# Storing a dense fallback's output from another DMA queue, in a kernel that takes the other branch

## The chip, the core and the metric

The kernel runs on one core of one Trainium2 chip. Its metric is the device time of one execution in microseconds (us), as the median of several runs. The core's engines, by the names that the profile uses, are PE (the matrix unit), PEld (its weight loads), DVE (the vector engine), ACT (the scalar engine), POOL (GpSimd) and SP (SyncE, which here only issues DMAs and waits). A name with a "q" behind it (POOLq, SPq) is that engine's sequencer, which runs waits, branches and the like.

## What is computed

Two graph layers on 3327 nodes with 512 features and a sparse symmetric adjacency matrix whose diagonal is one. Each layer adds its result to its input and normalises the rows. Layer 0 is graph attention with four heads; layer 1 mixes an attention sum with a plain neighbour sum through two gates:

```python
x, adj                                                # (3327, 512), (3327, 3327) of zeros and ones
# layer 0, for each head h
feats = x @ W[h]
logits = leaky_relu(e_self[:, None] + e_neigh[None, :], 0.2), adj == 0 masked
g0 = relu(softmax(logits) @ feats + b[h])
x = layernorm(x + g0)
# layer 1
h = x @ W_sa
e = where(adj != 0, exp(-leaky_relu(s_left[:, None] + s_right[None, :], 0.01)), 0)
x_a = (e / (e.sum(1) + 1e-5)) @ h
x_b = adj @ (x @ W_gcnb) + b_gcnb
g1 = sigmoid(attn_a * x_a + attn_b * x_b)             # attn_a, attn_b: sigmoids of row sums
x = layernorm(x + g1)
```

## The kernel before

The function `gat_then_gated_gnn` (L1445) has two ways to compute this. `sparse_pass` (L80) always runs. It turns each node's row of the adjacency matrix into a list of at most a few dozen neighbours, gathers those neighbours' rows and sums them with weights. While it does so it also tests whether the lists hold every neighbour; `covered` (L509) writes the answer into `flag`, a single word in on-chip memory (L523). Then comes `with tc.If(... flag ... > 0)` (L1450): if some list had overflowed, `dense_pass` (L1068) would compute everything anew from the whole matrix. With the inputs at hand the lists hold all neighbours, the flag is 0, and no instruction of `dense_pass` appears in the profile. It is a fallback that is built into the program and not run.

`sparse_pass` works on 26 tiles of 128 nodes. A first stage (until about 240 us in the profile) loads the adjacency matrix and the features from SP's queue, computes layer 0's feature rows (L351) into a table in DRAM, and makes the lists on DVE. A second stage (until about 660 us) is layer 0: POOL gathers table rows with indirect DMAs (L615), DVE and ACT weigh them, and PE sums them by multiplying with the identity (L763). The third stage is layer 1, with gathers again from L615, sums on DVE (L967) and PE (L988), and a projection (L1007). Finished rows are normalised on ACT (L1052, up to four tiles at a time) and put into the output with an indirect DMA from POOL, through this helper:

```python
def scatter(group, dst, rows, src, last=None):                    # L143
    put = nc.gpsimd.indirect_dma_start(                           # L145
        out=dst, out_offset=bass.IndirectOffsetOnAxis(ap=rows, axis=0), in_=src, in_offset=None,
        bounds_check=last, oob_is_err=last is None,
    ).ins
    ...
scatter("out", out, own(order[k]), z, N - 1)                      # L1055, 26 times
```

The order of the work is written out by hand, engine by engine; a layer above adds the semaphores. It counts each engine's finished instructions on one semaphore (`Pool_49`, `DVE_49` and so on), the DMAs issued by SP and ACT on eight semaphores `DMAHW0_49` to `DMAHW7_49` in turn, and the DMAs issued by POOL on eight more, `DMASW0_49` to `DMASW7_49`. Every finished DMA adds 16 to its semaphore.

Behind the branch the two ways join, and from there each semaphore must stand at the same value whichever way was taken. So the built program holds, beside the block with `dense_pass` (the true block), a second block that has no line of its own in the source (the false block; its instructions carry L1450). In it each engine adds to its semaphores what the true block would have added. For POOL the false block of the kernel before has seven instructions:

1. a semaphore instruction that waits until `Pool_49` reaches 63 and adds 67 to it;
2. four semaphore instructions that wait until `DMASW1_49` to `DMASW7_49` have reached the counts of all POOL DMAs issued so far;
3. an instruction that waits for `DMASW0_49` in the same way and then raises all eight, by 48 (six of them) or 64 (two). The profile calls it INC_SWDGE_SEM. (48 is three DMAs, 64 is four: 26 stores of `dense_pass`, L1442, dealt over eight semaphores.)
4. a branch to the block behind the join.

SP's false block has eight semaphore instructions, one for each of `DMAHW0_49` to `DMAHW7_49`; ACT, PE and DVE have one each.

The block behind the join (its instructions carry L1514) ends the program. SP waits for all sixteen DMA semaphores and the engines' own at their final values, runs two DRAIN instructions [...] and reports to a barrier. ACT, PE and DVE run a DRAIN and report too. POOL runs a DRAIN, collects the four reports, releases the others, runs a second DRAIN, clears the semaphores (EVENT_SEMAPHORE_RANGE_CLEAR), runs a third DRAIN and holds a second barrier of the same kind. Its end is the end of the execution.

Of the kernel before, what the change touches and what calls it, by code (L numbers as in the profile page):

```python
# [14 lines left out]
P = 128  # L15
# [1052 lines left out]
def dense_pass(  # L1068
# [21 lines left out]
    nc = tc.nc  # L1090
# [6 lines left out]
    def rows(t):  # L1097
        return min(P, N - t * P)
# [39 lines left out]
    x1 = x1_pool.tile([P, NT, F], F32, name="x1")  # L1138
# [25 lines left out]
    with tc.tile_pool(name="feats", bufs=1) as feats_pool:  # L1164
# [3 lines left out]
        with tc.tile_pool(name="p0", bufs=1) as p0, tc.tile_pool(name="p0s", bufs=2) as p0s, tc.tile_pool(  # L1168
# [16 lines left out]
            for c0 in range(0, N, CH):  # L1185
# [3 lines left out]
                for t in range(c0 // P, (c0 + cw + P - 1) // P):  # L1189
                    r, o = rows(t), t * P - c0  # L1190
# [19 lines left out]
            for t in range(NT):  # L1210
                r = rows(t)
# [24 lines left out]
        with tc.tile_pool(name="m0", bufs=2) as m0p, tc.tile_pool(name="m0o", bufs=1, space=PSUM) as pso, tc.tile_pool(  # L1236
            name="m0t", bufs=2, space=PSUM
        ) as pst:
            for n0 in range(0, N, NB):
# [3 lines left out]
                for j, t in enumerate(tiles):  # L1243
                    r = rows(t)
# [7 lines left out]
                for t0, g in groups(G):  # L1252
# [4 lines left out]
                    for t in range(t0, t0 + g):  # L1257
                        r = rows(t)
# [30 lines left out]
                for j, t in enumerate(tiles):  # L1289
                    r = rows(t)  # L1290
# [31 lines left out]
    with tc.tile_pool(name="p1", bufs=1) as p1, tc.tile_pool(name="p1s", bufs=2) as p1s, tc.tile_pool(  # L1322
# [19 lines left out]
        for t in range(NT):  # L1342
            r = rows(t)
# [24 lines left out]
    with tc.tile_pool(name="m1", bufs=2) as m1p, tc.tile_pool(name="m1o", bufs=1, space=PSUM) as pso, tc.tile_pool(  # L1368
        name="m1t", bufs=2, space=PSUM
    ) as pst:  # L1370
        for n0 in range(0, N, NB):
# [3 lines left out]
            for j, t in enumerate(tiles):  # L1375
                r = rows(t)
# [9 lines left out]
            for t0, g in groups(G):  # L1386
                at = m1p.tile([P, G, NB], F32, tag="at", name=f"at{n0}_{t0}")
                load_adjT(at, t0, g, n0, nw)
                for t in range(t0, t0 + g):
                    r = rows(t)  # L1390
# [22 lines left out]
            for j, t in enumerate(tiles):  # L1413
                r = rows(t)
# [24 lines left out]
            normalise(m1p, f"b{n0}", tiles, stats)  # L1439
            for t in tiles:  # L1440
                r = rows(t)
                nc.gpsimd.dma_start(out[t * P : t * P + r, :], x1[:r, t, :])  # L1442


def gat_then_gated_gnn(tc, x, xT, xB, xL, adj, adjT, adjB, adjL, diag, xo, W0, W0B, b0, a_self, a_neigh, *rest):  # L1445
    N = adj.shape[0]
    with tc.tile_pool(name="flag", bufs=1) as pool:
        flag = pool.tile([1, 1], I32, name="flag")
        sparse_pass(tc, flag, x, xB, xL, adjB, adjL, diag, xo, W0B, b0, a_self, a_neigh, *rest)
        with tc.If(tc.nc.values_load(flag[0:1, 0:1]) > 0):  # L1450
            dense_pass(tc, x[:N], xT, adj, adjT, W0, b0, a_self, a_neigh, *rest)
# [65 lines left out]
```

## Time and profile before

| what | us |
|---|---|
| median of three runs | 974.06 |
| lowest and highest of them | 973.56, 977.38 |
| the profiled execution's own time | 1108.9 |
| span of the profiled execution, first to last instruction | 1107.2 |

The profiled execution is longer than that median by 1108.9 - 974.06 = 134.8 us. All durations below come from it, and times of day ("at 1094") are microseconds from its start.

By stages the engines were busy as follows (us of busy time in the stage; the clock is what was granted to PE, as a share of full speed; the last column is the mean busy share of the core's DMA engines):

| stage | length | PE | DVE | ACT | POOL | clock | DMA |
|---|---|---|---|---|---|---|---|
| 0 to 240: lists and layer 0's features | 240.0 | 135.35 | 143.90 | 31.56 | 97.36 | 0.78 | 0.83 |
| 240 to 660: layer 0 | 420.0 | 326.46 | 233.34 | 135.87 | 252.84 | 0.85 | 0.62 |
| 660 to 720: layer 1 begins | 60.0 | 36.09 | 26.34 | 8.99 | 43.48 | 0.68 | 0.70 |
| 720 to 1094.9: layer 1 | 374.9 | 332.20 | 313.34 | 102.48 | 229.62 | 0.95 | 0.53 |

What is left, from 1094.9 to 1107.2, is the end of the program.

Three views of the profile are used below. The view by source line lists every kind of instruction that a line gave, on engines and sequencers, with its shortest, median and longest duration in ns and the start of the first and last of them in us. The view by windows gives the busy time and number of instructions of each engine in a stretch of time. The view of waits adds up who waited for whom; its releasers are inferred from semaphores.

### The profile page before, as it was taken

Reading aid. Unit: us, or ns where it says so; the run is one execution under the profiler, and the core shown is the slowest. Engines: PE = TensorE matmul, PEld = TensorE weight load, DVE = VectorE, ACT = ScalarE, POOL = GpSimd, SP = SyncE. Lnnn points to the kernel's source line nnn. Section 1 sums busy time; section 2 is a strip of 40 time slices with the busy share of each in tenths; the row PEclk is TensorE's granted clock in tenths of the full one; section 3 lists DMA queues with packets and bytes.
Section 4 is the critical chain, followed back from the end, with each engine's and each line's share of the span. In section 5 each row is a group of like instructions: output and inputs, shape, how many; then the busy total and the mean of one; then the engine's idle time right before and its main releaser. Section 6 shows DMA issues by size and latency. Waiting matters only on the chain.

```text
span 1107.2 us, 10091 instructions
## 1 busy us (share of the span) xinstructions
PE 830.1 (75%) x2534; PEld 435.9 (39%) x2534; DVE 716.9 (65%) x2118; ACT 278.9 (25%) x820; POOL 623.3 (56%) x664
## 2 busy tenths in 40 slices
PE   4499973028768697868848976689898989697992
PEld 3377751014334343434424432244344434343441
DVE  4286786187333673855536655398797989968872
ACT  1022120004221442433313421122222222131331
POOL 7410247607675466466766437737777777776311
PEclk9698995557778898989979985889898999898997
DMA  9899899603976567486766417726676576766200
GB/s 324 316 359 399 346 321 381 198 0 105 394 232 173 149 204 206 147 307 197 213 187 202 145 62 200 204 77 190 178 191 185 173 193 174 189 177 180 76 29 31
DMA packets 74243, 221.88 MB, mean 200 GB/s; under 512 B 14944, under 2 KB 19216, under 8 KB 73280
## 3 DMA queue, kind: packets, MB, share of 16 engines
q0 software_dynamic: 47008, 153.87, 47.1%
q1 hardware_dynamic: 24512, 65.17, 15.6%
q10 hardware_dynamic: 2656, 2.10, 0.6%
q8 instruction: 23, 0.38, 0.1%
q14 instruction: 44, 0.36, 0.1%
HBM read 200.01 MB, written 28.55 MB: 206 GB/s over the span
## 4 chain that ended last, share of the span: by engine, by line
PE 40%; issue 16%; POOL 12%; DVE 12%; another core or an unknown queue 9%; DMA 5%; ACT 5%; ACTq 0%; DVEq 0%; POOLq 0%; SPq 0%
PE acc L763 12%; PE pf L351 7%; POOL g L615 7%; PE po L1007 6%; PE acc L988 6%; PE pcol L787 2%; DMA g<-table,srt 2%; DMA at<-in_adjB 2%; PE acc L752 2%; DVE sw L967 2%; POOL out L145 1%; ACT g L758 1%; POOL lists L145 1%; PE pt L998 1%
## 5 line engine op out<-in xcount | busy, mean ns | idle before, releaser
L615 POOL DMA_INDIRECT g<-table,srt x464 | 476.1, 1026 | 217.9 <-issue 145.8
L763 PE MATMUL acc<-g,ident 128*128 128x512 f32 x504 | 238.3, 629 | 2.4 <-issue 2.4
L967 DVE SCALAR_TENSOR_TENSOR sw<-g,e,sw 128x512 f32<-128x512 f32 x226 | 169.4, 750 | 13.5 <-ACT sw L951 6.2
L763 PEld LDWEIGHTS acc<-g,ident 128*128 128x128 f32 x504 | 103.5, 206 | 139.8 <-issue 126.8
L988 PE MATMUL acc<-g,ident 128*128 128x512 f32 x262 | 126.4, 617 | 13.5 <-DMA g<-table,srt 9.5
L1007 PE MATMUL po<-wsa,sT 128*128 128x512 f32 x208 | 101.4, 633 | 18.3 <-issue 13.3
L351 PE MATMUL pf<-w,xc 128*128 128x260 f32 x416 | 103.4, 411 | 13.4 <-DVE w L291 13.4
L760 DVE TENSOR_TENSOR g<-g,w 128x512 f32<-128x512 f32 x176 | 109.7, 692 | 0.6
L351 PEld LDWEIGHTS pf<-w,xc 128*128 128x128 f32 x416 | 84.7, 206 | 29.4 <-DVE w L291 13.9
L1007 PE MATMUL po<-wg,sT 128*128 128x512 f32 x208 | 93.7, 593 | 0.0
L758 ACT ACTIVATE g<-g,w 128x128 f32<-128x128 f32 x304 | 91.9, 390 | 2.7 <-issue 2.2
L787 PE MATMUL pcol<-v,xt 128*128 128x8 f32 x208 | 35.7, 299 | 74.1 <-ACT xt L784 57.1
L988 PEld LDWEIGHTS acc<-g,ident 128*128 128x128 f32 x262 | 51.0, 197 | 82.6 <-issue 54.0
L1007 PEld LDWEIGHTS po<-wsa,sT 128*128 128x128 f32 x208 | 42.3, 206 | 77.3 <-issue 67.4
L969 DVE TENSOR_TENSOR g<-g 128x512 f32<-128x512 f32 x95 | 65.7, 692 | 3.3
L787 PEld LDWEIGHTS pcol<-v,xt 128*128 128x128 f32 x208 | 33.3, 244 | 80.6 <-ACT xt L784 62.0
L361 POOL DMA_DIRECT2D table<-row x26 | 14.4, 555 | 87.5 <-ACT st L360 87.5
L145 POOL DMA_INDIRECT out<-za,srt x26 | 28.8, 1108 | 57.2 <-ACT za L1052 51.1
L1007 PEld LDWEIGHTS po<-wg,sT 128*128 128x128 f32 x208 | 39.4, 190 | 48.8 <-issue 48.0
L1000 ACT COPY sT<-pt 128x512 f32<-128x512 f32 x52 | 29.1, 587 | 113.5 <-remote 56.7
L379 PE MATMUL pc<-at,pow 128*32 128x512 bf16 (+1 forms) x182 | 23.9, 434 | 36.7 <-DMA at<-in_adjB 20.2
L784 ACT COPY xt<-x1t 128x512 f32<-128x512 f32 x26 | 15.2, 584 | 141.0 <-PE x1t L780 74.9
(236 smaller groups left out, 934.3 us busy)
## 6 DMA issues: line engine op xcount, KB each, us to landing
at<-in_adjB SPq DMA_DIRECT2D x78, 512.0 KB
g<-table,srt POOLq DMA_INDIRECT x464
table<-row POOLq DMA_DIRECT2D x26, 260.0 KB
xc<-in_xB SPq DMA_DIRECT2D x6, 1024.0 KB
own<-in_xo SPq DMA_DIRECT2D x1, 3640.0 KB
own<-table SPq DMA_DIRECT2D x1, 3640.0 KB
at<-in_adjL SPq DMA_DIRECT2D x13, 256.0 KB
table<-x1a SPq DMA_DIRECT2D x12, 260.0 KB
```

The costliest lines, as they stand in the source:

```text
L145: put = nc.gpsimd.indirect_dma_start(out=dst, out_offset=bass.IndirectOffsetOnAxis(ap=rows, axis=0), in_=src, in_offset=None, bounds_check ...
L351: nc.tensor.matmul(pf[:, hh, :HC], xc[:, k, o : o + P], w0[:, k, hh, :], start=(k == 0), stop=(k == KT - 1))
L615: nc.gpsimd.indirect_dma_start(out=buf[:, q - q0, :], out_offset=None, in_=table[:, :], in_offset=bass.IndirectOffsetOnAxis(ap=srt[g][:, i ...
L758: nc.scalar.activation(gv[:, h, :], gv[:, h, :], AF.Copy, scale=w[:, s, h : h + 1])
L760: nc.vector.tensor_tensor(gv, gv, w[:, s, :].rearrange("p (h o) -> p h o", o=1).to_broadcast([P, H, FO]), ALU.mult)
L763: nc.tensor.matmul(acc, ident, buf[:, o + s - s0, 0:F], start=False, stop=(s == CAPS[j] and j not in T0))
L787: nc.tensor.matmul(pcol, xt1[:, k, :], v1[:, k, :], start=(k == 0), stop=(k == KT - 1))
L967: nc.vector.scalar_tensor_tensor(sw, g[:, i, 0:F], e[:, s : s + 1], sw, ALU.mult, ALU.add)
L969: nc.vector.tensor_add(g[:, i, 0:F], g[:, i - 1, 0:F], g[:, i, 0:F])
L988: nc.tensor.matmul(plain[j], to, row, start=(not sums_of_two and i == 0), stop=(sums_of_two and i == len(rows) - 1),)
L1000: nc.scalar.copy(sT, pt)
L1007: nc.tensor.matmul(proj[j], sT[:, k, :], wt[:, k, :], start=(half + k == 0), stop=(half + k == KT))
```

## The change

One call changes its engine. The 26 stores at the end of `dense_pass`, in the block that isn't run, are issued from SP's queue and no longer from POOL's:

```diff
@@ -1439,7 +1439,7 @@
             normalise(m1p, f"b{n0}", tiles, stats)
             for t in tiles:
                 r = rows(t)
-                nc.gpsimd.dma_start(out[t * P : t * P + r, :], x1[:r, t, :])
+                nc.sync.dma_start(out[t * P : t * P + r, :], x1[:r, t, :])
```

In the built program all that runs ahead of the branch is the same, instruction by instruction, on every engine. The true block loses 44 instructions on POOL and gains 42 on SP; the stores of one block of nodes stand on SP between the second and the third load of the next block's matrix tiles. In the false block POOL keeps the first of its seven instructions (`Pool_49` by 67, as before) and the branch; the four waits and INC_SWDGE_SEM are gone. SP's false block has the same eight instructions with other amounts (608 or 624 where it had 560 or 576). The block behind the join has the same 37 instructions; SP waits there for `DMASW0_49` to `DMASW7_49` at 1184 or 1200, which are the counts of the POOL DMAs that were issued, where it waited for 1232 or 1248.

## The prediction

> **What bounds the kernel now.** The change lies behind the last tile of layer 1, so I read the end of the program first. The view by windows, for all engines, from the last scatter on (columns: window, length, busy us and number of instructions of PE, PEld, DVE, ACT and POOL, granted clock, DMA share, GB/s):
>
> ```profile
> 1094.90:1096.80 1.90, 0.00 (x0) 0.00 (x0) 0.00 (x0) 0.00 (x0) 0.00 (x0) 0.50 0.39 146
> 1096.80:1097.30 0.50, 0.00 (x0) 0.00 (x0) 0.00 (x0) 0.00 (x0) 0.00 (x0) 0.50 0.05 16
> 1097.30:1099.20 1.90, 0.00 (x0) 0.00 (x0) 0.00 (x0) 0.00 (x0) 0.00 (x0) 0.50 0.01 4
> 1099.20:1106.30 7.10, 0.00 (x0) 0.00 (x0) 0.00 (x0) 0.00 (x0) 0.00 (x0) 0.50 0.00 0
> 1106.30:1107.20 0.90, 0.00 (x0) 0.00 (x0) 0.00 (x0) 0.00 (x0) 0.00 (x0) 0.50 0.00 0
> ```
>
> No engine works after 1094.9, and from 1097.3 no data moves: the last 10 us belong to sequencers. The view of the lines of branch and join, on POOL, says what its sequencer does there:
>
> ```profile
> L1450 POOLq EVENT_SEMAPHORE  x5: 17/42/43, 1096.9 to 1097.2; - x5
> L1450 POOLq TENSOR_LOAD <-flag x1: 507/507/507, 1093.6 to 1093.6; - x1
> L1450 POOLq COMPARE_BRANCH  x1: 53/53/53, 1094.2 to 1094.2; - x1
> L1450 POOLq INC_SWDGE_SEM  x1: 1916/1916/1916, 1097.3 to 1097.3; - x1
> ...
> L1514 POOLq EVENT_SEMAPHORE  x4: 17/17/17, 1106.4 to 1107.1; - x4
> L1514 POOLq DRAIN  x3: 46/103/7093, 1099.2 to 1106.9; - x3
> L1514 POOLq EVENT_SEMAPHORE_RANGE_CLEAR  x1: 177/177/177, 1106.7 to 1106.7; - x1
> ```
>
> INC_SWDGE_SEM takes 1.92 us, and the first DRAIN behind it 7.09 us (its longest of three; the others take 0.10 and 0.05). Together 9.0 us of POOL alone. Who waits for it, in the view of waits of SP's queue over the end:
>
> ```profile
> SPq L1514 <- DMA out<-za,srt: 435.8, 1, 435.8
> SPq L1514 <- PEq L1514: 7.1, 2, 6.6
> ```
>
> SP is through its false block at 663.3 and waits 435.8 us, until 1099.1. The view names the DMA of the last output rows, yet that had landed earlier: POOL's own waits for the same semaphores were over by 1097.3. What SP waits for from then on is the raise by INC_SWDGE_SEM, for it wants 1248 where the DMAs give 1200. Then SP stands 6.6 us at the barrier. The view names PE, which had reported at 1087.4; the one still missing is POOL, in its DRAIN. Last, the scatter that ends the real work, in the view in order of time:
>
> ```profile
> 1093.87 0.99 POOL L145 DMA_INDIRECT out<-za,srt  x1 [2.07 <-ACT za L1052]
> ```
>
> [...] The last scatter's record ends at 1094.86 and its last completion came at 1096.74, 1.88 us later[...] POOL's branch ends at 1094.27 and the next instruction runs at 1096.85: 2.6 us. [...]
>
> **The change, part by part.** I lay the tail out as it stands, from the trace, and then without the removed parts.
>
> Before: scatter landed 1096.74; POOL's five semaphore instructions 1096.85 to 1097.24; INC_SWDGE_SEM 1097.28 to 1099.20; SP's twelve waits and two DRAINs 1099.14 to 1099.96 (0.82 us), beside POOL's DRAIN, 1099.23 to 1106.32; then two barriers and the clearing, to 1107.17. From the release of POOL's wait for the reports to the end it is 0.80 us.
>
> *Removed: four semaphore waits* on POOL, 0.35 us (1096.96 to 1097.28, and the gap behind). They check what SP checks again.
>
> *Removed: INC_SWDGE_SEM*, 1.92 us, on both paths, SP's and POOL's. With it SP's start goes from 1099.14 to the landing, 1096.74 plus 0.04 (the gap between the raise at 1099.10 and SP's start) = 1096.78. SP then reports at 1096.78 + 0.82 = 1097.60.
>
> *The DRAIN.* It now stands behind one semaphore instruction at 1096.85 and begins at about 1096.9. Its length is not shown without the INC in front, so I bound it. Below: 0.05 us, the shortest of the three. Above: 7.09, as before. I take the low end, at most the 0.19 us of the DRAIN at the program's start with four memsets in front of it. The reason: before it lie only DMA instructions, and those free POOL at once. Scatters at 1089.52 and 1090.81 each took 0.99 and stood 0.30 apart; a POOL that were busy 10 us with what a scatter leaves behind could not do that. What else lies between the last scatter and the DRAIN is INC_SWDGE_SEM. Against that stands one thing: the program's first lines have an instruction of that name too,
>
> ```profile
> L1504 POOLq INC_SWDGE_SEM  x1: 27/27/27, 0.2 to 0.2; - x1
> ...
> L1504 POOLq DRAIN  x1: 188/188/188, 0.4 to 0.4; - x1
> ```
>
> and neither it nor the DRAIN behind it is long. But that one only resets, carries no amounts and names no semaphore, so I don't take it for the same work. So POOL is at the barrier by 1097.1 and waits there for SP.
>
> *Next to be late* is thus SP, with its 0.82 us behind the landing. The end: 1097.60 + 0.04 + 0.80 = 1098.44. The gain is 1107.17 - 1098.44 = 8.7 us, of which the INC and POOL's waits are 2.3 (1099.10 - 1096.78) and the DRAIN the other 6.4.
>
> *Added: other amounts* in SP's eight semaphore instructions. They ran from 662.8 to 663.3, 430 us ahead of the end; that wait covers them, and without cover they would cost what they did, 0.5 us.
>
> *Moved: 26 stores*, with their DMAs, to SP, ahead of the loads of the next block's third to last matrix tiles. Each waits for DVE to finish the normalisation, and those loads queue behind it, with PE and DVE waiting for the tiles. All of it is in the block that isn't run: cost nothing, because the flag is 0. If it were run, the price would be unknown from this trace. Nothing is moved ahead of the branch, so stages up to 1094.9 keep their time.
>
> Sum: -8.7 us against the profiled execution's own 1108.9, so 1100.2. The stretch holds no matrix work and next to no DMA, so I carry it over to the median in microseconds: 974.06 - 8.7 = **965.3**. If everything in the profiled execution were stretched by 1108.9 / 974.06, the gain would be 7.7 and the time 966.4.
>
> **Rivals.** *A, forecast: the DRAIN belongs to INC_SWDGE_SEM*, 965.3. *B: the DRAIN stays.* If the 7.09 us belong to the first DRAIN behind any POOL DMAs, or to the recording, then only 2.3 us are saved: in the first case the DRAIN runs from 1096.9 to 1104.0 and the program ends at 1104.8; 974.06 - 2.3 = 971.8. For it: the only other DRAINs of POOL stand before any DMA or right behind another DRAIN. Against it: no DMA is under way in those 7 us. *C: nothing is saved.* If POOL's cores were busy until 1106.3 with something that started with the last scatter, the DRAIN would start sooner and end at the same time: 974.1. Against it speaks the 0.30 us between scatters. *D, slower: instruction fetch.* POOL's program is 49 instructions shorter between branch and end[...]. Place: POOL, between branch and DRAIN, or inside the last block. Price: 2.6 us a fetch, as behind the branch now. It decides from the first additional fetch if the DRAIN stays (974.06 - 2.3 + 2.6 = 974.4), and only from the fourth if the DRAIN goes (4 x 2.6 = 10.4 against 8.7). For it: the branch does stall today. Against it: POOL's ten last instructions are few, and three instruction fetches of 8 KB are recorded from 1096.7 to 1097.5 without a stall of that size behind them.
>
> **How the numbers follow.** A 0.70, B 0.20, C 0.07, D 0.03. A's own range is 963.5 to 967.5 (both ways of carrying over, and run to run scatter: two of the three runs shown lie within 0.5 us and the third 3.3 above). The range reaches on over B, to 972.5, and leaves out C and D, about 0.10, and the tails. A change of 0.5%, 4.9 us, is about what a measurement of this kernel can tell from none. A is faster than that (below 969.2); B, C and D lie within it: faster 0.70, same 0.28, and slower 0.02 for a D of several fetches.
>
> **What would show it.** In the profile after: no INC_SWDGE_SEM at L1450 and one semaphore instruction of POOL there; SP's wait for the output's DMA ending within 0.1 us of the landing; all three DRAINs of POOL under 0.2 us; 1.7 us from landing to end, where it was 10.4. A DRAIN of 7 us in the profile means B, whether or not the median moves as in A; a DRAIN that still ends some 9.6 us after the landing means C; a gap well over 2.6 us behind POOL's branch, or a new one further on, means D. Short DRAINs with a median near 972 would say that the 7 us were the recording's. Any difference ahead of the branch would contradict the whole reading.

## The result and the profile after

The changed kernel takes 970.57 us (median of 20 runs, 967.71 to 974.86) where the kernel before takes 974.23 (median of 20, 971.03 to 977.38). The ratio is 0.9965 with a 95% interval of 0.9953 to 0.9978: 3.4 us faster, 2.1 to 4.6. The forecast was 8.7 us.

One thing has to be known to read the traces: chips differ. On two of the chips used in the experiments the kernel before takes 975 to 978 us, on three others 1104 to 1108. Going by their lengths, the profiled execution shown before the change ran on a chip of the slower kind, the first profile after on one of the faster. So I compare tails, from the start of the last output scatter to the end of the program. The changed kernel's tail didn't depend on the chip: it was 8.93 us in a run of 969.5 us span and 8.93 us again in one of 1094.8. The scatter from which it counts, in the first of them:

```profile
960.57 0.98 POOL L145 DMA_INDIRECT out<-za,srt  x1 [2.07 <-ACT za L1052]
```

Before the change the tail was 1107.17 - 1093.87 = 13.30 us. It is thus 4.4 us shorter, within the interval of the measured gain.

The same views as before the change. The view by windows, from the start of POOL's first closing DRAIN on (busy us and number of instructions of PE, PEld, DVE, ACT, POOL, then clock, DMA share, GB/s):

```profile
961.50:963.70 2.20, 0.00 (x0) 0.00 (x0) 0.00 (x0) 0.00 (x0) 0.05 (x1) 0.50 0.35 129
963.70:964.60 0.90, 0.00 (x0) 0.00 (x0) 0.00 (x0) 0.00 (x0) 0.00 (x0) 0.50 0.00 0
964.60:968.70 4.10, 0.00 (x0) 0.00 (x0) 0.00 (x0) 0.00 (x0) 0.00 (x0) 0.50 0.00 0
968.70:969.50 0.80, 0.00 (x0) 0.00 (x0) 0.00 (x0) 0.00 (x0) 0.00 (x0) 0.50 0.00 0
```

The scatter has landed by 963.72 and SP is through with its waits by 964.6; then 4.1 us pass in which no engine works and no data move. POOL's sequencer, by the lines of the branch and of the join:

```profile
L1450 POOLq TENSOR_LOAD <-flag x1: 503/503/503, 960.3 to 960.3; - x1
L1450 POOLq COMPARE_BRANCH  x1: 50/50/50, 960.9 to 960.9; - x1
L1450 POOLq EVENT_SEMAPHORE  x1: 17/17/17, 961.4 to 961.4; - x1
...
L1514 POOLq EVENT_SEMAPHORE  x4: 17/17/17, 968.7 to 969.4; - x4
L1514 POOLq DRAIN  x3: 50/109/7158, 961.5 to 969.2; - x3
L1514 POOLq EVENT_SEMAPHORE_RANGE_CLEAR  x1: 177/177/177, 969.0 to 969.0; - x1
```

INC_SWDGE_SEM and the four waits are gone, as announced. The DRAIN is not: it takes 7.16 us with no INC_SWDGE_SEM in front of it. And the first instruction behind the branch comes 0.44 us after it (960.96 to 961.40), where it had come after 2.59. The view of waits of SP's queue over the end:

```profile
SPq L1514 <- DMA out<-za,srt: 398.3, 1, 398.3
SPq L1514 <- PEq L1514: 4.8, 2, 4.3
```

The first line now means what it says: SP waits for the landing, until 963.74. The second is again the barrier, where the one missing is POOL, still in its DRAIN: 4.3 us, where it had been 6.6.

### The profile page after: what moved, and what is told of

It reads as the page before. It is cut to its first block, busy times and chain, and to the rows that moved or that the text cites. A ratio compares the mean times of both kernels' runs of the same rounds, so it can differ in the third digit from the quotient of the medians.

```text
span 969.5 us, 10086 instructions
## 1 busy us (share of the span) xinstructions
PE 804.4 (83%) x2534; PEld 421.7 (43%) x2534; DVE 716.6 (74%) x2118; ACT 278.2 (29%) x820; POOL 626.2 (65%) x664
## 4 chain that ended last, share of the span: by engine, by line
PE 45%; DVE 19%; DMA 12%; POOL 11%; issue 7%; ACT 4%; DVEq 0%; ACTq 0%; POOLq 0%
PE acc L763 21%; PE pf L351 9%; POOL g L615 7%; DMA g<-table,srt 7%; DVE sw L967 7%; DMA at<-in_adjB 3%; PE po L1007 3%; PE pcol L787 3%; PE acc L988 3%; PE acc L752 3%; DVE g L969 2%; ACT xt L784 1%; DMA a_row<-in_a_self 1%; PE x1t L780 1%; POOL sprod L321 1%
## 5 line engine op out<-in xcount | busy, mean ns | idle before, releaser
L763 PE MATMUL acc<-g,ident 128*128 128x512 f32 x504 | 230.8, 614 | 1.4 <-DVE g L760 1.4
L763 PEld LDWEIGHTS acc<-g,ident 128*128 128x128 f32 x504 | 100.4, 199 | 132.1 <-issue 101.1
L988 PE MATMUL acc<-g,ident 128*128 128x512 f32 x262 | 128.6, 618 | 24.9 <-DVE g L969 14.7
L1007 PE MATMUL po<-wg,sT 128*128 128x512 f32 x208 | 98.0, 616 | 0.0
L1007 PE MATMUL po<-wsa,sT 128*128 128x512 f32 x208 | 95.2, 601 | 0.3 <-ACT sT L1000 0.3
L988 PEld LDWEIGHTS acc<-g,ident 128*128 128x128 f32 x262 | 49.1, 193 | 95.8 <-issue 44.7
L1037 ACT ACTIVATE za<-za 128x512 f32<-128x512 f32 x26 | 16.4, 631 | 170.8 <-DVE za L1035 170.8
L1007 PEld LDWEIGHTS po<-wsa,sT 128*128 128x128 f32 x208 | 40.2, 194 | 51.3 <-issue 48.9
L787 PE MATMUL pcol<-v,xt 128*128 128x8 f32 x208 | 32.4, 283 | 33.1 <-ACT xt L784 33.1
L787 PEld LDWEIGHTS pcol<-v,xt 128*128 128x128 f32 x208 | 30.0, 222 | 38.8 <-ACT xt L784 38.6
L717 DVE TENSOR_TENSOR w<-g,srt 128x20 f32<-128x20 f32 (+3 forms) x55 | 9.7, 184 | 48.2 <-DMA g<-table,srt 46.9
```

The lines of the kernel that those rows point to most:

```text
L763: nc.tensor.matmul(acc, ident, buf[:, o + s - s0, 0:F], start=False, stop=(s == CAPS[j] and j not in T0))
L787: nc.tensor.matmul(pcol, xt1[:, k, :], v1[:, k, :], start=(k == 0), stop=(k == KT - 1))
L988: nc.tensor.matmul(plain[j], to, row, start=(not sums_of_two and i == 0), stop=(sums_of_two and i == len(rows) - 1),)
L1007: nc.tensor.matmul(proj[j], sT[:, k, :], wt[:, k, :], start=(half + k == 0), stop=(half + k == KT))
```

## The experiments

The theory at this point: a DRAIN on POOL works off something that POOL's own DMAs leave behind. Rivals: it has a fixed price behind any POOL DMA; or the first long one in a program pays for something loaded once; or, as forecast, it belongs to INC_SWDGE_SEM.

### One DRAIN more, early (e1, g3)

```diff
                 scatter("out", out, own(order[k]), z, N - 1)
+            if k0 == 20:
+                nc.gpsimd.drain()
             ready = None
```

> The changed kernel with one DRAIN more on POOL, behind the scatters of tiles 20 to 22 of layer 1's order, where POOL then idles about 12 us; three scatters follow it. Backlog theory (a DRAIN works off something that POOL's DMAs leave behind, so its length grows with the DMAs since the last DRAIN): the early DRAIN takes about 7.1 us, hidden, the closing one under 0.5 us, the end comes about 2 us behind the last landing; 4.1 us faster than the changed kernel, near 966.5. Fixed-price theory (the first DRAIN behind any POOL DMA takes 7.1 us): both take 7.1 us, no gain, near 970.6. Once-only theory (the first long DRAIN of the program pays for something loaded once): the same time as the backlog theory.

Timed twice, the second time on a chip of the faster kind:

> The changed kernel with the early DRAIN, the fastest form so far, timed once more. Tail from the start of the last scatter 4.7 us where the kernel before has 13.3: 8.6 us, 0.8 to 0.9%, faster than before. If the early DRAIN costs something elsewhere (it keeps POOL until 9 us after the scatters in front of it), the gain is smaller and the span ahead of the last scatter longer.

Ratios to the kernel before: 0.9907 (0.9861 to 0.9953) and 0.9930 (0.9908 to 0.9951; 968.19 us against 974.83). The tail is 4.67 and 4.58 us. The second run's DRAINs on POOL, by source line:

```profile
L1057 POOLq DRAIN  x1: 9247/9247/9247, 941.4 to 941.4; - x1
...
L1516 POOLq DRAIN  x3: 50/109/2163, 961.3 to 964.6; - x3
```

and the last scatter ahead of the early one:

```profile
942.85 0.98 POOL L145 DMA_INDIRECT out<-za,srt  x1 [0.30 <-ACT sp L1027]
```

The early DRAIN takes 9.25 us. Its record starts at 941.4, while POOL still has two of the three scatters ahead of it to issue; from the end of the last of these (943.84) it is 6.86 us to the DRAIN's own end at 950.7, well before POOL's next scatter at 955.99. The closing DRAIN takes 2.16 us, and that is its wait for the last scatter: it ends 0.17 us after the landing at 963.26. SP's waits say the same, 0.5 us at the first barrier:

```profile
SPq L1516 <- DMA out<-za,srt: 395.8, 1, 395.8
SPq L1516 <- PEq L1516: 0.7, 2, 0.5
```

The fixed price is out: a DRAIN with DMAs in front of it can be short. The last scatter stood at 960.3 of the span, as in the changed kernel (960.6), so the early DRAIN cost nothing visible. This form has the shortest tail of all that ran.

### The same with INC_SWDGE_SEM (e4)

The same edit in the kernel before.

> The kernel before (with INC_SWDGE_SEM) with the same early DRAIN. Backlog theory: the closing DRAIN is under 0.5 us and INC_SWDGE_SEM, if it goes through the same backlog, falls from 1.9 us to well under 1 us; about 8 us faster than before, near 966.3, so the change is worth next to nothing beside an early DRAIN. Once-only theory: the DRAIN is short, INC_SWDGE_SEM stays at 1.9 us; 6.4 us faster than before, near 967.8. If the 7.1 us of the DRAIN belong to INC_SWDGE_SEM, as the prediction had it, or are a fixed price: no gain, near 974.2.

```profile
L1452 POOLq INC_SWDGE_SEM  x1: 260/260/260, 1086.2 to 1086.2; - x1
...
L1516 POOLq DRAIN  x3: 46/103/302, 1086.5 to 1087.8; - x3
```

INC_SWDGE_SEM 0.26 us instead of 1.92, the DRAIN behind it 0.30 instead of 7.09. This is what the forecast excluded: the instruction to which it gave the 7 us is there, and the DRAIN is short. As both became short by the same edit, I take INC_SWDGE_SEM to have been long for the same reason as the DRAIN. The tail is 5.22 us: 8.1 us shorter by one DRAIN more, without the change. Beside an early DRAIN the whole change is worth 0.6 us (5.22 against 4.58 or 4.67). The ratio to the kernel before is 0.9840 (0.9754 to 0.9926), from six runs that lie 21 us apart on a chip of the slower kind: faster, but the size can't be told from it.

### The branch's stall (e5, g2)

```diff
                 nc.sync.dma_start(out[t * P : t * P + r, :], x1[:r, t, :])
+        pad = m1p.tile([P, 44], F32, name="pad", bufs=1)
+        for i in range(44):
+            nc.gpsimd.memset(pad[:, i : i + 1], 0.0)
```

These memsets lie in the block that isn't run; they stand for the 44 instructions of POOL that left it, so that it has 198 again, as before the change. POOL executes none of them.

> The changed kernel with 44 small memsets on POOL at the end of the block that isn't run, so that POOL's false block stands where it stood before the change; the instructions that run are those of the changed kernel. Fetch theory (part of the gain is a shorter stall behind POOL's branch, 0.5 us where it was 2.6, because the code behind the branch came to lie elsewhere): the stall is 2.6 us again, the DRAIN starts and the program ends 2.1 us later than in the changed kernel, near 972.7. Rival (the shorter stall comes from the missing semaphore waits or from chance): near 970.6.

```profile
L1453 POOLq COMPARE_BRANCH  x1: 53/53/53, 1090.7 to 1090.7; - x1
L1453 POOLq EVENT_SEMAPHORE  x1: 17/17/17, 1093.6 to 1093.6; - x1
...
L1517 POOLq DRAIN  x3: 50/103/7093, 1093.7 to 1101.3; - x3
```

The stall is back, 2.77 us, and the tail is 11.18 us, 2.25 more than the changed kernel's. With 22 memsets, to see whether the stall goes in a step or grows with the length of the block:

> The changed kernel with 22 small memsets in the block that isn't run, half of the earlier padding. [...] it is one of the two values seen, 0.4 or 2.6 to 2.8 us. If it grows with the distance, it lies between, near 1.6 us. The closing DRAIN is 7.1 us either way.

The stall was 0.44 us and the tail 8.93: at these three lengths of the block a step, not a slope. In all traces taken, the stall was 2.55 to 2.83 us where POOL's true block had its old 198 instructions, and 0.44 us with 154 or 176.

What the long stall waits for is not shown, though. In all nine traces that have it, the first instruction behind the branch ran 0.11 to 0.14 us behind the landing of the last scatter (in the padded kernel at 1093.58, the landing at 1093.46). That instruction does not ask for the landing: it waits for `Pool_49` alone, and in the six traces with the short stall it ran 2.1 to 2.3 us ahead of it. So the prediction's price of 2.6 us a fetch stays an estimate, which no run shows, and what held POOL until the scatter had landed stays open.

The medians of this group can't carry as much. On the chips of the slower kind, runs of one kernel scatter widely (before: 1093.56 to 1128.88), and the padded kernel came out at 0.9902 (0.9866 to 0.9939) of before, though its tail accounts for only 2.1 us, 0.2%. The rest lies ahead of the last scatter, where the instructions are the same. I can't explain it, so the argument rests on the tails. The changed kernel timed again there:

> The changed kernel itself, timed on the same chip as the experiments if it falls there. Tail from the start of the last scatter to the end: 8.9 us, POOL's stall behind the branch 0.4 us, closing DRAIN 7.1 us, as in its first profile; so 4.4 us (0.4%) faster than before, 2.2 us faster than the padded kernel and 4.3 us slower than the one with the early DRAIN, as far as the scatter of times on this chip lets it be seen.

0.9956 (0.9897 to 1.0015), with a tail of 8.93 us, a stall of 0.44 and a DRAIN of 7.17: consistent, but too wide to say more.

### What the DRAIN works off (e2, f2 to f4, g1, g4, h1)

> The changed kernel with four DRAINs more on POOL: behind its first 10 DMAs, behind 51 more, behind 282 more at the end of layer 0, and the early one of the first experiment behind 251 more; 3 DMAs follow. Backlog theory: lengths rise with these counts, roughly 0.3, 1 to 1.5, 7, 7 and under 0.5 us, or level off where the backlog has a limit. Once-only theory: the first takes 7 us, all others under 0.5. Fixed-price theory: all five about 7.1 us. The time itself is not to be compared, since three of these DRAINs stand where POOL is needed.

The time from each DRAIN's start to the last landing, and from there to its end, in us:

| POOL DMAs since the last DRAIN | length | to the landing | behind it |
|---|---|---|---|
| 10 | 8.97 | 8.51 | 0.46 |
| 51 | 10.87 | 8.73 | 2.14 |
| 282 | 8.34 | 4.38 | 3.96 |
| 251 | 5.78 | 4.15 | 1.63 |
| 3 | 2.41 | 2.25 | 0.16 |

A price paid once doesn't fit the second and third row, a fixed one doesn't fit the last column; but here the work runs beside landings, so that its length can't be read directly. So the next kernels are the kernel before, in which POOL has waited for all landings ahead of INC_SWDGE_SEM, each with one DRAIN more at another place (the edit is the one line `nc.gpsimd.drain()`; at the end of layer 0 for 254, at four places in layer 1 for 120, 37, 79 and 112, ahead of layer 0's gathers for 536).

> The kernel before with one DRAIN more on POOL at the end of layer 0, so that 254 of its 597 DMAs lie behind it. In this kernel POOL waits for all landings ahead of INC_SWDGE_SEM, so both it and the closing DRAIN meet landed DMAs alone. Backlog in proportion to the DMAs since the last DRAIN: INC_SWDGE_SEM about 1.0 us and the closing DRAIN about 3.1 us (7.09 for 597, 0.30 for 3). Backlog that is full long before that: 1.9 and 7.1 us, as before.

> The same with the DRAIN moved into layer 1, so that 120 DMAs lie behind it. In proportion: INC_SWDGE_SEM about 0.6 us, closing DRAIN about 1.6 us. A backlog that levels off below 120: 1.9 and 7.1 us.

> The same with 37 DMAs behind the DRAIN. In proportion: INC_SWDGE_SEM about 0.36 us, closing DRAIN about 0.7 us. A backlog that levels off below 37: 1.9 and 7.1 us. If it levels off between two of these counts, the DRAIN rises faster than in proportion to 597: at 37, for instance, to more than 0.7 us.

254 gave 1.04 and 3.48 us, near proportion; 120 gave 0.48 and 1.20; but 37 gave 0.94 and 3.08, more than 120. Proportion fell. What remained striking was that INC_SWDGE_SEM and the DRAIN moved together, along one straight line. That suggested a sawtooth as an estimate of what is left: it grows by one entry with each DMA, and from time to time some 106 entries go at once. The entry is a unit of this estimate, worked out from the lengths; no trace shows one.

> The kernel before with a DRAIN more on POOL in layer 1, so that 79 DMAs lie behind it. Sawtooth theory (the backlog grows by one entry a DMA, 0.082 us of DRAIN each, from 0.30 us at 3 to 3.08 at 37, and POOL clears it by itself whenever some 106 have piled up, so that 120 left 14 and 254 left 42): closing DRAIN about 6.5 us, INC_SWDGE_SEM about 1.8 us, both far above what 120 DMAs gave. Proportional theory, with 37 as an accident: DRAIN 0.8 to 1.0 us, INC_SWDGE_SEM about 0.4 us.

> The kernel before with a DRAIN more on POOL ahead of layer 0's gathers, so that 536 DMAs lie behind it. Sawtooth theory with 106 to a period (536 is five periods and 6): closing DRAIN about 0.5 us and INC_SWDGE_SEM about 0.3 us, though 536 is nearly all of the 597; if the 14 gathers of double rows in layer 0 count for more than one entry each, up to 14 entries more, 1.7 us and 0.6 us. If the length simply follows the number of DMAs once it is large: near 6.4 us and 1.8 us.

79 gave 1.78 and 6.51 us, as the sawtooth said. 536 gave 2.44 and 9.20, which none of my three numbers had. If 106 go at a time but only when more than 112 are there, then 536 = 4 x 106 + 112, and 112 DMAs alone must give the same:

> The kernel before with a DRAIN more on POOL in layer 1, so that 112 DMAs lie behind it, all of layer 1's kind. If POOL clears about 106 entries at a time, but only once more than 112 have piled up (536 = 4 x 106 + 112, 120 = 106 + 14): closing DRAIN about 9.2 us and INC_SWDGE_SEM about 2.4 us, far above the 1.20 and 0.48 us that 120 DMAs gave. If it clears at 106, as I had it at first: 0.30 + 3 x 0.082 = 0.5 us and 0.3 us, and the 9.2 us behind 536 DMAs have another cause.

They did. The lines of 120, 79 and 112 DMAs, in this order, show it: the most DMAs of the three have the shortest DRAIN, about a fifth and an eighth of the others.

```profile
L1452 POOLq INC_SWDGE_SEM  x1: 480/480/480, 1115.0 to 1115.0; - x1
...
L1516 POOLq DRAIN  x3: 46/103/1201, 1115.5 to 1117.3; - x3
```

```profile
L1452 POOLq INC_SWDGE_SEM  x1: 1780/1780/1780, 967.5 to 967.5; - x1
...
L1516 POOLq DRAIN  x3: 46/103/6509, 969.3 to 976.4; - x3
```

```profile
L1452 POOLq INC_SWDGE_SEM  x1: 2435/2435/2435, 967.6 to 967.6; - x1
...
L1516 POOLq DRAIN  x3: 46/103/9200, 970.0 to 979.8; - x3
```

All together, with the tail from the last scatter's start:

| DMAs since the last DRAIN | left of them by the sawtooth | INC_SWDGE_SEM | closing DRAIN | tail |
|---|---|---|---|---|
| 3 | 3 | 0.26 | 0.30 | 5.22 |
| 37 | 37 | 0.94 | 3.08 | 8.33 |
| 79 | 79 | 1.78 | 6.51 | 12.56 |
| 112 | 112 | 2.44 | 9.20 | 16.00 |
| 120 | 14 | 0.48 | 1.20 | 5.96 |
| 254 | 42 | 1.04 | 3.48 | 9.04 |
| 536 | 112 | 2.44 | 9.20 | 15.89 |
| 597 (kernel before) | 86, from its DRAIN | 1.92 | 7.09 | 13.30 |

From the rows of 3 and 112 I estimate an entry at (9.20 - 0.30) / 109 = 0.082 us of the DRAIN and (2.44 - 0.26) / 109 = 0.020 us of INC_SWDGE_SEM.

*Where the work starts.* When only the last few DMAs are still under way, the lengths fit if a DRAIN's work is counted from the end of POOL's last DMA instruction ahead of it, with the landings beside it. With 597 DMAs and the last scatter under way the DRAIN ended 7.10 us after that instruction in three traces (the changed kernel twice, and with 22 memsets), 4.9 to 5.1 us behind the landing; with all landed it took 7.09 us (the kernel before and the padded one). The 282 DMAs of layer 0 in the table of four DRAINs took 5.77 us counted so: by the estimate 70 entries, and 282 - 2 x 106 is 70. The 251 took 3.39, where 251 - 2 x 106 = 39 entries give 3.25. Where the work is short, as in the closing DRAIN of the first experiment, the DRAIN ended with the landing (0.17 us behind it). The rows of 10 and 51, whose last landings came 7.9 and 5.2 us after that instruction, can't be read in this way.

*The last row.* 597 - 5 x 106 is 67, not 86. The added DRAINs themselves, each in a kernel that has only one, and counted in the same way, say where the 19 come from. In the run with 79 DMAs it stands behind the first 518; POOL's last instruction ahead of it, and the DRAIN:

```profile
807.17 0.98 POOL L145 DMA_INDIRECT out<-za,srt  x1 [0.30 <-ACT sp L1027]
```

```profile
L1057 POOLq DRAIN  x1: 16970/16970/16970, 800.5 to 800.5; - x1
```

From 808.15 to 817.46 it is 9.31 us, by the estimate 113 entries. Behind the first 343, 477, 485, 560 and 594 DMAs it was 3.67, 5.96, 6.61, 4.08 and 6.86 us: 44, 72, 80, 49 and 83 entries. Each is the number of DMAs plus 19, less a multiple of 106, and so is 86. Since 536 DMAs behind the first 61 left 112 without the 19, these belong, by the estimate, to the first 61, many of which have other shapes; which of them count for more than one entry isn't shown (the DRAIN added right behind them waited for landings, too). And as 113 were still there, the estimate's limit is 113, not 112. The clearing itself is inferred from what was left: no record of POOL shows it. Nor do these runs tell DMAs from rows, as all 536 have 128 rows.

## Why the prediction was wrong

*Where the end is lost: right.* The last 10 us were sequencers' work, POOL held the barrier, and the names that the view of waits gave (a DMA, then PE) were both wrong in the way that was said.

*INC_SWDGE_SEM and the waits: right.* Forecast for them alone 2.3 us; the padded kernel, which has the change without the shorter stall, has a tail 13.30 - 11.18 = 2.1 us shorter, and from the landing to the end it is 10.43 - 8.13 = 2.3.

*The DRAIN: wrong*, and this is the step that failed. "I take the low end" of 0.05 to 7.09 us, because POOL is free 0.3 us after a scatter and "INC_SWDGE_SEM is" what else lay in between. The first half is true and proves nothing: in the profile after, two scatters stood 0.30 us apart again, and the DRAIN took 7.16 us. So 6.4 us of the forecast were not there. The bound from above was the true one. The DRAIN's length went with the DMAs since the DRAIN before it (86 entries here, by the estimate), with INC_SWDGE_SEM (7.09 us) or without (7.16). That the early INC_SWDGE_SEM and its DRAIN were short was explained away by its other mode; the simpler reading was that no DMA stood before them.

*Next to be late is SP: wrong* as long as the DRAIN stays. With the early DRAIN it was right: there the end came 1.66 us behind the landing, and 1.7 was forecast.

*Rival B: the DRAIN stays, right; its cause, half right.* Its layout, 1104.8 - 1096.74 = 8.06 us from the landing to the end, is that of the padded kernel, 8.13. But the 7 us do not belong to "the first DRAIN behind any POOL DMAs": with three DMAs behind the last DRAIN it was 0.30. "Against it: no DMA is under way in those 7 us" was no argument: with all DMAs landed the DRAIN took 9.20 us behind 112 of them and 0.30 behind three. The other form, the recording's, isn't needed; no run here tests it. That the median came near B's 971.8 is in part luck, as B did not foresee the shorter stall.

*Rival C: out.* The DRAIN ended 4.9 us behind the landing, not 9.6.

*Rival D: right place, wrong sign.* That POOL's block became shorter did matter, but the stall fell, from 2.59 to 0.44 us; and 2.6 us as the price of a fetch is not shown. Before the change a shorter stall would have gained nothing: POOL's next waits were for the landing, which came at 1096.74, 0.11 us ahead of the stall's end. Without those waits the stall sets when the DRAIN starts, and the prediction kept it as it was. Sum: 2.1 + 2.25 = 4.4 us, the whole difference of the tails; the measured gain of 3.4 (2.1 to 4.6) contains it.

*That SP's new amounts cost nothing: right.* Its eight instructions ran from 564.9 to 565.5, 398 us ahead.

*Carrying over:* the 1108.9 was most likely another chip, as each chip on record kept to one kind; for the tail, microseconds were the right unit.

*The landing's 1.88 us:* the scatter's packets moved from 1095.42 to 1096.35 in that time, and the last completion came 0.39 us behind them. And the recorded time of a DRAIN is not all its own work: the 2.16 us of the closing one, with the early DRAIN, were the wait for a landing.

## What to carry to other kernels

A block that isn't run can still cost time, through what the other branch must make up for (2.1 us of the tail here) and through its length (2.25 us); read the sequencers' rows behind the last data movement. If the program ends in a DRAIN of GpSimd behind many of its own DMAs, put one more DRAIN into a stretch in which GpSimd idles near the end: here that alone shortened the tail by 8.1 us, the change alone by 4.4. Only few DMAs may follow it: with 112 behind it the tail grew to 16.0 us. And when a long instruction has two possible owners, the undisturbed lengths elsewhere don't settle it; give both weight in the forecast until a trace has one without the other.

## What the runs showed of the hardware

- A DRAIN on POOL did not end ahead of the landing of POOL's last DMA: with three DMAs since the DRAIN before, it ended 0.17 us behind it. With all DMAs landed it took 0.30 us for 3, 3.08 for 37, 6.51 for 79 and 9.20 for 112; my estimate from 3 and 112 is 0.082 us a DMA. With 597 DMAs and the last scatter under way it ended 7.10 us behind POOL's last DMA instruction, beside the landing. INC_SWDGE_SEM rose with it, from 0.26 us for 3 to 2.44 for 112, by estimate 0.020 us a DMA.
- Behind indirect DMAs of 128 rows the length didn't rise on and on: 112 gave 9.20 us, 120 gave 1.20, 254 gave 3.48 and 536 again 9.20. So the closing DRAIN was 8 us shorter with eight DMAs more behind the DRAIN before it. A sawtooth that drops by 106 DMAs, each time that more than 113 would be left, fits these lengths; it is an estimate from them, and no record shows a drop.
- A taken branch on POOL stalled either 0.44 or 2.55 to 2.83 us, according to the length of the block that it jumps over (154 or 176 instructions, or 198). The long stall ended 0.11 to 0.14 us behind the landing of the last scatter in all nine traces that have it.
